# Cross-attention block on one core: scores taken two pairs at a time, context fetched in pieces, the last two pairs' context products placed among output products, and moments turned on chip before they are stored

## The chip, the cores and the metric

The kernel runs on one core of one Trainium2 chip. The metric is the time of one execution in microseconds on the device, as a median over runs. A core has TensorE (PE in the profile, with its weight loads as PEld), VectorE (DVE), ScalarE (ACT), GpSimd (POOL) and SyncE (SP). In this kernel SP issues nearly all the DMAs.

## The reference

A gated cross-attention block followed by a gated feed-forward layer with low-rank adapters. B is 32 sequences, S is 64 tokens, the width is 512, and there are 32 heads of 128.

```python
def xattn(hidden_q, hidden_kv, mask, bias, Wq, Wk, Wv, Wo):
    q, k, v = [(h @ W).reshape(32, 64, 32, 128) for h, W in ((hidden_q, Wq), (hidden_kv, Wk), (hidden_kv, Wv))]
    score = einsum('bqhd,bkhd->bhqk', q, k) / sqrt(128) + bias
    probs = where(mask, softmax(where(mask, score, -inf)), 0)
    return einsum('bhqk,bkhd->bqhd', probs, v).reshape(32, 64, 4096) @ Wo

x = x + tanh(g_xattn[0]) * xattn(layernorm(x), ctx, mask, bias, Wq, Wk, Wv, Wo)
x = x + tanh(g_ffn[0]) * (layernorm(x) @ weight.T + bias_ffn + adapter(layernorm(x)))
```

## The kernel before

Matrix products are done in three terms of rounded halves: each operand is split into a high part (cast by ACT) and a low part (a subtraction on POOL or DVE), and `mm3` (line 98) multiplies high by high, high by low and low by high. The three large projections use a scheme with seven block products in place of eight (`unit`).

The 2048 tokens are worked in two phases of 1024 (`NPH`, index `p`). A phase has two stages. `stage_a` computes K for 16 pairs of heads (`NPR`), then V in four groups; both are stored to DRAM (`kd`, `vd`). Beside it, it takes the moments of the layer norm of x (`x_stats`), stores them with `x_spread` (lines 575 and 576: mean and reciprocal deviation, one float per token, so that a later load can broadcast them along the partitions), and prepares the turned x. `attention` then goes through the 16 pairs in `run`. For pair n it does:

- `unit` on the query weights: seven products of six matmuls, 128x512 each. The results go to `qT`, by ACT copies and DVE additions (lines 354, 359, 376);
- `pv(n - 1)`: the context of the pair before, `po` (line 823), from V and the turned probabilities `pt`. ACT casts it to `ch`, DVE writes the rest `cl` (lines 826, 827);
- `scores(n)`: 64 small matmuls into `ps` (line 765). DVE scales and adds the bias and takes the maximum (767, 769), POOL subtracts the maximum (770), ACT takes the exponential (771);
- `softmax(n)`: DVE sums and inverts (786 to 788), POOL multiplies (789), DVE transposes in blocks of 32 (781), and ACT copies the 16 blocks into `pt` (798);
- `oproj(n - 1, t)`: for eight token tiles, six matmuls 128x512 of `ch` and `cl` with the output weights `wo` into `pa`. DVE adds this to `acc` (847).

Query weights of the next pair are split by `prep`, output weights by `prep_o`, and the mask is added to the bias by `bias_mask` (726). These are Python generators in a list `streams`; each `beat()` after a product issues one step of every one of them, and `drain` issues what is left of one. So the order of instructions on each engine is written by hand (the pool context is under a manual schedule)[...]. Buffers of `big` are named slots: `res[0]` to `res[6]` and `rest`. K of a pair has one slot, V of two pairs has two, `wo` has one, `pt` has one. `sm` (scores of a pair) has two, used by even and odd pairs. [...]

At the end of a phase the last `oproj`s are mixed with other work. In phase 0 this is the first half of phase 1's first K (`plain_half`, `ppk` in the profile), ahead of the last context product. In phase 1 it is the first FFN chunk: `between(t)` puts the FFN's transposes (`tpf`) and their split (`fa`, lines 989 and 990) between output tiles, and `ffn_chunk(0)` begins with the adapter product `pt<-fa,a` (`ffn_lora`, lines 997 and 998). `pt<-tp` is the probabilities and `pt<-fa,a` the adapter product; they share only the name.

## Time and profile before

| what | value |
|---|---|
| runs | 1538.19 us median of 3 (1537.93 to 1539.19) |
| profiled execution, its own time | 1539.96 us |
| its span | 1538.0 us, granted TensorE clock 1.000 |
| PE busy | 1528.1 us (99%), 9000 matmuls |
| DVE, ACT, POOL busy | 963.8, 721.2, 1019.3 us |
| DMA | 248.49 MB, mean 162 GB/s |
| one pair of steady attention, from one `po` to the next | 26.23 us |

Times in the views are microseconds from the start of the span. The busy share of PE is a share of occupied time, and not of peak. In the chain of waits, rows of one engine stand one after the other as they set the end; each row has its start, its length, and how many instructions are merged in it. A row of PE's waits has the instruction, what released it, the total, the number of times and the longest. A timeline row has start, length, engine, line, operation, output and inputs, shapes and count, and in brackets the engine's idle time before and what ended it.

### The profile page before, as it was taken

The page shows a single profiled execution, that of the slowest core. Times are in us where ns is not written, and L with a number is a line of the kernel's source. Part 1 is how long each engine was busy: PE and PEld are TensorE (multiplying, and loading weights), DVE is VectorE, ACT ScalarE, POOL GpSimd, SP SyncE. Part 2 cuts the span into 40 slices and gives each one's busy share as a digit, 9 for nine tenths or more (in the row PEclk, how much of TensorE's full clock was granted, in tenths as well). Part 3 has the DMA queues.
Part 4 walks back from the last instruction along what each step waited for, and adds up shares of the span by engine and source line. Part 5 has one row for each costly group of instructions (what it writes and reads, how often), then busy time and mean ns, then how long its engine had stood idle before and what let it go on. Part 6 is the DMA issues. An engine that isn't in the chain of part 4 may idle for free.

```text
span 1538.0 us, 24845 instructions
## 1 busy us (share of the span) xinstructions
PE 1528.1 (99%) x9000; PEld 1286.0 (84%) x9000; DVE 963.8 (63%) x1595; ACT 721.2 (47%) x1594; POOL 1019.3 (66%) x1128
## 2 busy tenths in 40 slices
PE   9999999999999999999999999999999999999998
PEld 7888888888888888888887888888888888888887
DVE  5665554386666767575675558438666676757764
ACT  6444233345555555556444423334555555555521
POOL 3889478966666657574687947896666665757410
PEclk9999999999999999999999999999999999999999
DMA  5764544384243424441566454438424342444211
GB/s 210 270 183 160 199 164 166 140 298 158 85 176 138 178 83 179 180 152 67 212 240 192 151 199 165 166 137 296 163 85 176 138 176 85 175 182 153 75 42 69
DMA packets 86301, 248.49 MB, mean 162 GB/s; under 512 B 14145, under 2 KB 15169, under 8 KB 77986
## 3 DMA queue, kind: packets, MB, share of 16 engines
q1 hardware_dynamic: 85890, 246.38, 44.6%
q8 instruction: 71, 1.16, 0.3%
q10 hardware_dynamic: 288, 0.52, 0.1%
q14 instruction: 52, 0.43, 0.1%
HBM read 173.45 MB, written 73.42 MB: 161 GB/s over the span
## 4 chain that ended last, share of the span: by engine, by line
PE 93%; DMA 3%; DVE 2%; POOL 1%; issue 1%; ACT 0%; SPq 0%; ACTq 0%; DVEq 0%; POOLq 0%
PE pa L98 22%; PE po L823 7%; PE pzv L98 6%; PE pvv L98 6%; PE pxv L98 6%; PE pzq L98 5%; PE pxq L98 5%; PE pvq L98 5%; PE pzk L98 4%; PE pvk L98 4%; PE pxk L98 4%; PE ps L765 4%; PE pyv L98 3%; PE ppk L98 3%; PE pf L98 3%; PE pyq L98 2%
## 5 line engine op out<-in xcount | busy, mean ns | idle before, releaser
L98 PE MATMUL pa<-wo,ch 128*128 128x512 f32 x1024 | 320.2, 394 | 0.0
L798 ACT COPY pt<-tp 32x256 f32<-32x256 f32 x496 | 200.3, 404 | 87.1 <-DVE tp L781 76.0
L90 POOL TENSOR_TENSOR wo<-rawo,wo 128x512 fp32r<-128x512 f32 x64 | 81.1, 1286 | 224.7 <-ACT wo L89 217.0
L98 PEld LDWEIGHTS pa<-wo,ch 128*128 128x128 f32 x1024 | 189.6, 188 | 39.8
L847 DVE TENSOR_TENSOR acc<-pa,acc 128x512 f32<-128x512 f32 x256 | 170.1, 673 | 79.4 <-PE pa L98 79.3
L98 PE MATMUL pa<-wo,cl 128*128 128x512 f32 x512 | 200.0, 391 | 0.0
L823 PEld LDWEIGHTS po<-pt,v 128*128 128x128 f32 x1024 | 119.1, 192 | 2.6
L827 DVE TENSOR_TENSOR cl<-po,ch 128x512 fp32r<-128x512 f32 x128 | 88.3, 692 | 52.5 <-ACT ch L826 52.0
L823 PE MATMUL po<-pt,v 128*128 128x128 f32 x1024 | 119.4, 275 | 0.0
L98 PEld LDWEIGHTS pa<-wo,cl 128*128 128x128 f32 x512 | 96.2, 188 | 20.6
L826 ACT CAST ch<-po 128x512 fp32r<-128x512 f32 x128 | 74.8, 586 | 71.2 <-PE po L823 70.6
L354 DVE TENSOR_TENSOR vt<-pvv,vt 128x512 f32<-128x512 f32 x64 | 44.1, 689 | 91.5 <-PE pvv L98 91.4
L771 ACT ACTIVATE sm<-sm 128x512 f32<-128x512 f32 x64 | 40.5, 633 | 123.0 <-POOL sm L770 123.0
L770 POOL TENSOR_TENSOR sm<-sm,mx 128x512 f32<-128x512 f32 x64 | 66.9, 1048 | 46.3 <-DVE mx L769 46.3
L354 DVE TENSOR_TENSOR kT<-pvk,kT 128x512 f32<-128x512 f32 x56 | 38.5, 688 | 67.1 <-PE pvk L98 67.1
L376 ACT COPY vt<-pxv 128x512 f32<-128x512 f32 x32 | 18.8, 588 | 131.0 <-PE pxv L98 131.0
L726 POOL TENSOR_TENSOR sm<-sm,madd 128x512 f32<-128x512 f32 x60 | 76.3, 1292 | 1.8 <-DMA sm<-bias 1.8
L789 POOL TENSOR_TENSOR sm<-sm,r 128x512 f32<-128x512 f32 x64 | 66.9, 1045 | 14.5 <-DVE r L788 11.1
L354 DVE TENSOR_TENSOR qT<-pzq,qT 128x512 f32<-128x512 f32 x64 | 44.3, 692 | 38.0 <-PE pzq L98 37.4
L765 PE MATMUL ps<-kB,qT 128*64 128x64 f32 x2048 | 67.2, 224 | 0.3 <-DVE qT L354 0.3
L765 PEld LDWEIGHTS ps<-kB,qT 128*64 128x64 f32 x2048 | 62.5, 138 | 4.9 <-issue 0.7
L354 DVE TENSOR_TENSOR qT<-pvq,qT 128x512 f32<-128x512 f32 x64 | 44.1, 690 | 35.5 <-PE pvq L98 35.5
(975 smaller groups left out, 3698.9 us busy)
## 6 DMA issues: line engine op xcount, KB each, us to landing
kd<-kT SPq DMA_DIRECT2D x64, 512.0 KB, 3.3
vd<-vt SPq DMA_DIRECT2D x128, 256.0 KB, 2.4
kB<-kd SPq DMA_DIRECT2D x32, 1024.0 KB, 4.9
v<-vd SPq DMA_DIRECT2D x32, 1024.0 KB, 9.0
rawq<-wq SPq DMA_DIRECT2D x32, 512.0 KB, 4.6
sm<-bias SPq DMA_DIRECT2D x64, 256.0 KB, 5.2
rawo<-wo SPq DMA_DIRECT2D x32, 512.0 KB, 3.3
rawk<-wk SPq DMA_DIRECT2D x31, 512.0 KB, 5.4
```

The costliest lines, as they stand in the source:

```text
L90: eng.tensor_tensor(lo, raw, hi.bitcast(F32), ALU.subtract)
L98: nc.tensor.matmul(ps, a, b, start=start and i == 0, stop=stop and i == 3 * n - 1, skip_group_check=True)
L354: nc.vector.tensor_tensor(o, ps, i, ALU.add)
L726: nc.gpsimd.tensor_tensor(t, t, masks[p][0], ALU.add)
L765: nc.tensor.matmul(ps[h * S:(h + 1) * S, t, :], qT[:, i, tok], kT[:, i, tok], start=True, stop=True)
L770: nc.gpsimd.tensor_tensor(s, s, mx.unsqueeze(2).to_broadcast([P, NT, S]), ALU.subtract)
L789: nc.gpsimd.tensor_tensor(ss[i], ss[i], r.unsqueeze(2).to_broadcast([P, NT, S]), ALU.mult)
L798: f(pt[dst, i, :, src], of[src, :, ki * 32:(ki + 1) * 32])
L823: nc.tensor.matmul(ps[:, t * P:(t + 1) * P], b["v", n // 2][c][:, t, hg * P:(hg + 1) * P], pt[:, i, c * 4 + t, :], start=True, stop=True)
L826: nc.scalar.copy(ch[:, i, sl], ps)
L827: nc.vector.tensor_tensor(cl[:, i, sl], ps, ch[:, i, sl].bitcast(F32), ALU.subtract)
L847: nc.vector.tensor_tensor(acc[t], ps, acc[t], ALU.add)
```

## The change

Scores of pairs 0 and 1 stay alone. From pair 2 on, `score(a, a + 1)` takes the scores of two pairs in a row; between two such groups stand two `oproj`s, two query `unit`s and two `pv`s, each whole. The exponential becomes a stream step of its own, `normed` and `turned` are the two halves of the old softmax, and for the odd pair of a group they run apart. K has two slots, V has one slot that holds one pair and is loaded anew for each. The last two pairs have `last_turned`: a second tile of probabilities (`pz`), and context products cut in halves (`pv(n, (0,))`, `pv(n, (1,))`) that stand between output tiles, around `fill()`: half a K in phase 0, the first FFN chunk in phase 1. The output weights of pair 14 get a slot of their own. `load_ctx`, `ffn_fetch` and `x1_load` become generators that issue one DMA at a time. `x_spread` turns the moments on DVE and stores them in runs of 32 floats. FFN rows rotate through other buffers. In the diff, cut to its core, the removed lines of the old loop and softmax are left out where they stand in the listing above.

```diff
     def x_spread(p):
         mv, y = mvx[p], rx[p]
-        nc.sync.dma_start(out=lnd[p][0].rearrange("(t q) -> q t", q=P), in_=mv[:, :, 0])
-        nc.sync.dma_start(out=lnd[p][1].rearrange("(t q) -> q t", q=P), in_=y)
+        m, mt = [st.tile([P, 4, NT], F32, tag=f"m{i}", name=f"m{i}{p}", bufs=1) for i in range(2)]
+        for i in range(4):
+            nc.vector.tensor_copy(m[:, i], y if i % 2 else mv[:, :, 0])
+        nc.vector.transpose(mt.rearrange("p a b -> p (a b)"), m.rearrange("p a b -> p (a b)"))
+        for i in range(4):
+            nc.sync.dma_start(out=lnd[p].rearrange("s t (b q) -> b (s t) q", b=4)[i],
+                              in_=mt[i * 32:i * 32 + 2 * NT].rearrange("p a b -> p (a b)"))
...
         def load_k(n):
-            b["k", n] = big(res[1], [P, 2, TP], F32, f"kB{p}_{n}")
+            b["k", n] = big(res[1 + n % 2], [P, 2, TP], F32, f"kB{p}_{n}")
             nc.sync.dma_start(out=b["k", n], in_=kd[p][n])
 
-        def load_v(q):
-            b["v", q] = [big(res[2 + c], [P, 4, 512], F32, f"v{p}_{q}_{c}") for c in range(2)]
-            for c in range(2):
-                nc.sync.dma_start(out=b["v", q][c], in_=vd[p][q][:, c * 4:(c + 1) * 4, :])
+        def load_v(n):
+            b["v", n] = big(res[3], [P, NT, 256], F32, f"v{p}_{n}")
+            nc.sync.dma_start(out=b["v", n], in_=vd[p][n // 2][:, :, n % 2 * 256:(n % 2 + 1) * 256])
...
             load_k(0)
             load_v(0)
+            load_bias(1)
+            load_k(1)
...
             nc.gpsimd.tensor_tensor(s, s, mx.unsqueeze(2).to_broadcast([P, NT, S]), ALU.subtract)
+            beat()
+            if n:
+                streams.append(exped(s))
+            else:
+                nc.scalar.activation(s, s, AF.Exp)
+
+
+        def exped(s):
             nc.scalar.activation(s, s, AF.Exp)
-            beat()
-
...
+        def normed(n, wait):
+            for _ in range(wait):
+                yield
             for i in range(2):
-                nm = f"{p}_{n}_{i}"
-                r = st.tile([P, NT], F32, tag="r", name=f"r{nm}")
-                nc.vector.tensor_reduce(r, ss[i], AX.X, ALU.add)
+                t = sm[n % 2][:, i]
+                r = st.tile([P, NT], F32, tag="r", name=f"r{p}_{n}_{i}")
+                nc.vector.tensor_reduce(r, t, AX.X, ALU.add)
                 nc.vector.reciprocal(r, r)
                 nc.vector.tensor_tensor(r, r, masks[p][1], ALU.mult)
-                nc.gpsimd.tensor_tensor(ss[i], ss[i], r.unsqueeze(2).to_broadcast([P, NT, S]), ALU.mult)
-                if alone and i:
-                    turn(0)
-                yield
-            quads = [(h, qi, ki) for h in range(2) for qi in range(2) for ki in range(2)]
-
-            def copy(f, i, of, h, qi, ki):
-                src = slice(h * 64 + qi * 32, h * 64 + qi * 32 + 32)
-                dst = slice(h * 64 + ki * 32, h * 64 + ki * 32 + 32)
-                f(pt[dst, i, :, src], of[src, :, ki * 32:(ki + 1) * 32])
-
-            if alone:
-                for k, q in enumerate(quads):
-                    copy(nc.scalar.copy, 0, tp[0], *q)
-                    copy(nc.vector.transpose, 1, ss[1], *q)
-                    if k % 3 == 2:
-                        yield
-                return
+                nc.gpsimd.tensor_tensor(t, t, r.unsqueeze(2).to_broadcast([P, NT, S]), ALU.mult)
+                yield
...
+        def turned(n, pace=(1, 2, 2, 3, 2, 2, 2, 2)):
+            tp = []
             for i in range(2):
-                turn(i)
-                yield
+                tp.append(rows.tile([P, NT, S], F32, tag="row", name=f"tp{p}_{n}_{i}"))
+                turn(tp[i], n, i)
+                yield
+            if n + 2 < NPR:
+                load_bias(n + 2)
+                b["m", n + 2] = bias_mask(n + 2)
+                streams.append(b["m", n + 2])
...
+        def last_turned():
+            n = NPR - 2
+            z = kqp.tile([P, 2, NT, S], F32, tag="kq", name=f"tz{p}")
+            tp = [rows.tile([P, NT, S], F32, tag="row", name=f"tp{p}_{n}_{i}") for i in range(2)]
+            pts.append(big(res[1], [P, 2, NT, P], F32, f"pz{p}"))
+            yield from normed(n, 0)
+            for i, _ in enumerate(normed(n + 1, 0)):
+                turn(tp[i], n, i)
+                yield
+            todo = [(n, i, q) for i in range(2) for q in quads]
+
+            def copies(k):
+                for m, i, q in todo[:k]:
+                    copy(nc.scalar.copy, m, i, tp[i] if m == n else z[:, i], *q)
+                del todo[:k]
+
+            for i in range(2):
+                turn(z[:, i], n + 1, i)
+                copies(3)
+                yield
+            for h in range(2):
+                nc.vector.memset(pts[1][h * S:(h + 1) * S, :, :, (1 - h) * S:(2 - h) * S], 0.0)
+                copies(3)
+                yield
+            copies(4)
+
+            def rest():
+                todo.extend((n + 1, i, q) for i in range(2) for q in quads)
+                while todo:
+                    copies(4)
+                    yield
+            b["s", n + 1] = rest()
+            streams.append(b["s", n + 1])
...
+        def pv(n, cs=(0, 1)):
+            drain(b["s", n])
+            for c in cs:
+                for i in range(2):
+                    ps = psum(f"po{p}_{n}_{i}_{c}")
+                    for t in range(4):
+                        nc.tensor.matmul(ps[:, t * P:(t + 1) * P], b["v", n][:, c * 4 + t, i * P:(i + 1) * P],
+                                         pts[n > NPR - 2][:, i, c * 4 + t, :], start=True, stop=True)
+                    sl = slice(c * 512, (c + 1) * 512)
+                    nc.scalar.copy(ch[:, i, sl], ps)
+                    nc.vector.tensor_tensor(cl[:, i, sl], ps, ch[:, i, sl].bitcast(F32), ALU.subtract)
+                    beat()
+            if cs[-1] == 1 and n + 1 < NPR:
+                load_v(n + 1)
+                if ("n", n + 1) in b:
+                    drain(b["n", n + 1])
+                    b["s", n + 1] = turned(n + 1)
+                    next(b["s", n + 1])
+                    next(b["s", n + 1])
+                    streams.append(b["s", n + 1])
...
             raw = raw_of.pop(("o", p * NPR + n))
-            t = big(res[4], [P, 2, 1024], F32R, f"wo{p}_{n}")
+            t = big(res[2 if n == NPR - 2 else 4], [P, 2, 1024], F32R, f"wo{p}_{n}")
...
+            def score(*ns):
+                for n in ns:
+                    drain(b.get(("m", n)))
+                for n in ns:
+                    for i in range(2):
+                        scores(n, i, qT[n], b["k", n])
+                for n in ns:
+                    if n + 2 < NPR:
+                        load_k(n + 2)
+                n = ns[0]
                 if n == 0:
-                    enter_late()
+                    b["s", n] = both(normed(n, 0), first_turned())
+                elif n == NPR - 2:
+                    b["s", n] = last_turned()
                 else:
-                    drain(soft)
-                if 0 < n < NPR - 1:
-                    qb = prep("q", g + 1, nc.gpsimd, 2, 4)
-                    streams.append(qb)
-                if n:
-                    pv(n - 1)
-                    drain(ob)
-                for i in range(2):
-                    scores(n, i, qT, b["k", n])
-                if n + 1 < NPR:
-                    load_k(n + 1)
-                    load_bias(n + 1)
-                    if n % 2 == 0 and n:
-                        load_v(n // 2)
-                soft = softmax(n, None if n == 0 else (1, 2, 2, 3, 2, 2, 2, 2) if n < NPR - 1 or between else (4,) * 4)
-                streams.append(soft)
-                if n:
-                    for t in range(NT - 2):
-                        oproj(n - 1, t)
-                        if n == NPR - 1 and between:
-                            between(t)
-                    drain(qb)
-                    if n + 2 < NPR:
-                        fetch("q", g + 2, "r0")
-                    elif n + 2 == NPR:
-                        before_last()
-                if n == NPR - 5:
-                    prefetch()
-            ob = prep_o(n)
-
-            def finish():
-                oproj(n - 1, NT - 2)
-                oproj(n - 1, NT - 1)
-                streams.append(ob)
-
-            def attend():
-                drain(soft)
-                drain(ob)
-                pv(n)
-            last(finish, attend, lambda t: oproj(n, t), acc)
+                    b["s", n] = both(normed(n, 1), turned(n))
+                streams.append(b["s", n])
+                if 1 < n < NPR - 2:
+                    b["n", n + 1] = normed(n + 1, 5)
+                    streams.append(b["n", n + 1])
+
+            q_unit(0)
+            enter_late()
+            b["m", 1] = bias_mask(1)
+            score(0)
+            streams.append(b["m", 1])
+            start_o(0)
+            q_unit(1)
+            pv(0)
+            start_q(2, nc.gpsimd)
+            score(1)
+            oproj(0)
+            drain(qb[2])
+            fetch("q", p * NPR + 3, "r0")
+            q_unit(2)
+            start_o(1)
+            pv(1)
+            q_unit(3)
+            score(2, 3)
+            for a in range(4, NPR, 2):
+                drain(qb[a])
+                fetch("q", p * NPR + a + 1, "r0")
+                oproj(a - 3)
+                q_unit(a)
+                start_o(a - 2)
+                pv(a - 2)
+                q_unit(a + 1)
+                oproj(a - 2)
+                start_o(a - 1)
+                pv(a - 1)
+                score(a, a + 1)
+                if a == NPR - 8:
+                    streams.append(paced(prefetch(), 4))
+
+            n = NPR - 1
+            oproj(n - 2, range(4), between)
+            fill()
+            oproj(n - 2, range(4, 6))
+            start_o(n - 1)
+            pv(n - 1, (0,))
+            oproj(n - 2, range(6, NT))
+            pv(n - 1, (1,))
+            start_o(n)
+            oproj(n - 1, range(4))
+            drain(ob[n])
+            freed()
+            pv(n, (0,))
+            oproj(n - 1, range(4, NT))
+            pv(n, (1,))
+            last(lambda t: oproj(n, range(t, t + 1)), acc)
...
+            def fill():
+                nonlocal kt0
                 g = (p + 1) * NPR
-                finish()
-                fetch("k", g + 1, "r1")
                 kt0 = k_tile(g)
                 while (2, 1) not in first[1]:
                     next(fb)
                 plain_half(wt["k", g], first[1], k_dst(kt0), f"k{g}", 0)
...
+            def freed():
+                fetch("k", (p + 1) * NPR + 1, "r1")
                 gate.append(True)
...
             def between(t):
-                if 1 <= t < 5:
-                    ffn_tile(0, t - 1)
+                ffn_tile(0, t)
                 if t == 2:
                     ffn_norm(1, 0)
 
-            def last(finish, attend, o, acc):
+            def fill():
+                drain(weights)
+                ffn_chunk(0, first=False)
+
```

## The prediction

> **What bounds the kernel now.** I read the busy times first, then the chain of waits in order of time, then PE's own waits, then the timeline at the places that the change touches.

> ```profile
> PE 1528.1 (99%) x9000; PEld 1286.0 (84%) x9000; DVE 963.8 (63%) x1595; ACT 721.2 (47%) x1594; POOL 1019.3 (66%) x1128
> ```

> PE is busy for 99% of the span, so there is no idle time to win in the middle, only the cost of PE's own work. The chain shows that this cost depends on what follows what (start, length, engine, tile, instructions):

> ```profile
> 683.57 8.41 PE pa L98 x36
> 698.77 2.72 PE pa L98 x12
> 704.21 3.57 PE po L823 x32
> 707.78 2.01 PE ps L765 x64
> 709.80 11.13 PE pa L98 x48
> 720.93 5.44 PE ppk L98 x24
> 726.37 3.57 PE po L823 x32
> 729.94 10.90 PE pa L98 x48
> ```

> The reader is to compare the `pa` rows. Twelve take 2.72 us: 0.2267 us each. 36 should take 8.16 and take 8.41, 48 should take 10.88: behind scores (`ps`) they take 11.13, behind the context product (`po`) 10.90. A change from scores to output products costs 0.25 us, one from `po` to them 0.02. All that PE waited for, beyond a few tenths at the starts, are two waits:

> ```profile
> PE pyk L98 <- POOL wk27p L299: 1.3, 1, 1.3
> PE pt L998 <- DVE fa L990: 1.0, 1, 1.0
> ```

> The first has its cause here (SPq issues; ACT's idle time is in brackets): a 512 KB key weight, issued just ahead of the two DMAs of the moments, lands 12.2 us later.

> ```profile
> 826.84 0.74 SPq L264 DMA_DIRECT2D rawk<-wk  x1
> 827.63 1.19 SPq L575 DMA_DIRECT2D lnd<-mv  x1
> ...
> 839.11 0.41 ACT L295 CAST wk27p<-rawk 128x256 fp32r<-128x256 f32 x1 [6.49 <-DMA rawk<-wk]
> ```

> The others show what one softmax costs its helpers at the end of phase 0, and how DVE's queue held PE before the adapter product of phase 1:

> ```profile
> 716.85 0.70 DVE L781 STREAM_TRANSPOSE tp<-sm 128x512 f32<-128x512 f32 x1
> 717.64 6.82 ACT L798 COPY pt<-tp 32x256 f32<-32x256 f32 x16 [3.10 <-DVE tp L781]
> 725.23 2.51 POOL L90 TENSOR_TENSOR wo<-rawo,wo 128x512 fp32r<-128x512 f32 x2 [7.72 <-issue]
> ```

> ```profile
> 1443.12 0.68 DVE L767 SCALAR_TENSOR_TENSOR sm<-ps,sm 128x512 f32<-128x512 f32 x1
> ...
> 1454.26 0.68 DVE L990 TENSOR_TENSOR fa<-tpf,fa 128x512 fp32r<-128x512 f32 x1
> 1454.99 0.50 PE L998 MATMUL pt<-fa,a 128*128 128x512 f32 x1 [1.03 <-DVE fa L990]
> ```

> ```profile
> kB<-kd SPq DMA_DIRECT2D x32, 1024.0 KB, 4.9
> v<-vd SPq DMA_DIRECT2D x32, 1024.0 KB, 9.0
> ```

> [...]the four `fa` subtractions stand between softmax work in DVE's order, and PE waits for the last. [...]the 4 KB moments, one float at a time, took about 13 us to land. [...]V's new loads have pieces of 1 KB, and no load of before has both that and this size.

> **The change, part by part**, against the profiled span of 1538.0 us. (That execution took 1539.96 in all; the runs' median is 1538.19, 0.2 above the span, so I add the sum to it.)

> *Grouped scores.* Seven groups a phase, 14 in all. Each merges two entries to scores and two exits. An exit costs 0.25. Entry: score starts come 59 ns apart by twos, so 64 are 1.89 us, and the chain gives 2.02: 0.13. The first context product of a group now leads to query products instead: 0.02 back. 14 x 0.36 = **-5.1 us**.

> *Moments turned.* Four copies of 128x8 and one small transpose on DVE (0.15 to 0.7 each; DVE waits for PE here 0.6 at a time) and four DMAs of 128-byte pieces in place of two of 4-byte ones. The weight then lands some 5 us after issue and PE's wait goes: 1.3, with the restart **-1.7 us**. In phase 0 the same delay meets no PE wait.

> *Bit-by-bit fetches* (context, FFN weights, x1) and other buffers for FFN rows: same bytes, needed 30 us later, and a row's store (2.0 us) ends before its buffer's next use 3.7 us on; **0**, hidden by the query and output products; bounds -0.5 and +0.5.

> *Steady groups.* Let T be the end of a group's scores. The even pair's turned weights are wanted at T + 10.9 (outputs) + 9.5 (query) + 0.25 = T+20.7, its second head 0.9 later. DVE: eight score passes at 0.66 from 1.4 us after the first score: done T+2.8. Sums, normalising, transposes between the `acc` additions: second transpose T+9.6. ACT's 16 copies at 0.427 lie between query copies and casts, the last of them behind a POOL sum that stands after the bias additions: T+20.2. **0 us**, with 1.3 us to spare. Wo, bias, K and V have 7 to 40 us.

> *Starts.* Wo's cast and subtraction (1.3 on POOL) now come between pair 0's two normalisings, its last transposes behind, and PE loses two waits for qT of 0.4. Some 0.5 us late in each phase: **+1.0** (bounds -1.5, +4).

> *End of phase 0.* Here the cover shrinks: pair 14's context comes 13.9 us after T (four outputs, 5.44 of key product, two outputs) instead of 20.7, with pair 15's softmax interleaved on DVE. DVE: score passes T+2.8, then four times `acc` 0.67 and a sum with its reciprocal 1.04, a transpose 0.70 in the third and fourth: first transpose T+8.6, second T+11. (Pair 15's transposes and two fills of zeros come later on DVE, where nothing waits for them.) ACT: 16 copies and two key copies (0.58) from T+8.7: T+16.7. PE reaches the second head at 14.8: **+2.0**. Behind this ACT has pair 15's 16 copies, interleaved with context casts and the casts of Wo 14: the second cast ends T+24.2, POOL's second half (1.26) T+25.5. PE wants it at T+23.2 by then, counting the first wait: **+2.4**. The fetch of Wo 15 waits on SP for that POOL instruction (it reads the buffer), and V 15 is queued behind it, since V has one buffer and is loaded only after pair 14's last product. [...]PE needs it after the last 0.5 of output tile 0 and three more at 1.36, 4.6 in all: **+2.1** (0 to 4, as V lands in 4.9 to 7.3).

> *End of phase 1.* The adapter product now follows output tile 3 and its FFN tile directly; before, three output tiles lay between. S is the start of the scores. DVE, in its order: eight passes from S+1.4 to 6.7; `acc` and sum to 8.4; the first `fa` subtraction waits for ACT's four exponentials and cast, 9.2 to 9.9; then three times 0.67 + 1.04 + 0.67, two transposes 1.4, one FFN norm 0.54: S+19.0. PE is there at S + 3.9 + 0.25 + 4 x (1.36 + 0.48) = S+11.5, one product later stands: **+7.2** (5 to 8.5), in place of the old wait of **-1.3**. The FFN chunk then hides pair 14's copies; Wo 14 is late by **+0.9**, V 15 as above **+2.1**.

> Sum: -5.1 - 1.7 + 1.0 + 2.0 + 2.4 + 2.1 + 7.2 - 1.3 + 0.9 + 2.1 = **+9.6 us**, so **1547.8**.

> **The rivals.** (1) *The ends keep up* (faster): it takes an ACT and DVE that run ahead of my queues. For it: in the old phase 0 the 16 copies ended at 724.46, 1.5 us before use. Against: twice the softmax stands in less time. It decides where all waits of ends and starts fall under 5 us; with only 1 us in all: -5.1 - 1.7 - 1.3 + 1 = 1531. (2) *Half of it*: the adapter wait only 5, the chain of Wo 14 and V 15 within its cover: -8.1 + 1 + 2 + 5 = about 1538, no change. (3) *The steady groups stall too*: a bias that lands over a microsecond late holds POOL, its sum, ACT's cast and the last copies; 0.8 us in each of 12 groups gives 1557. (4) *Merging saves less than it says*: if query products after `po` cost 0.25 like outputs after scores, the gain is 14 x 0.13, and the time 1551.

> **How the numbers follow.** 0.2% is 3.1 us, about what a measurement of this kernel can tell from no change. My forecast has 0.64 (own range 1541.5 to 1554), rival 1 has 0.13, rival 2 0.10, rival 3 0.08, rival 4 0.05. Faster 0.13; same 0.09 (most of rival 2); slower 0.78. To hold 8 in 10 the range goes from 1535, below rival 2, to 1556, short of the worst of rival 3.

> **What would show it.** Right: scores of 128 in one block with 0.25 after them once in two pairs; no wait of `pyk`; a PE wait of `pt` for DVE's `fa` of 5 us or more; PE waits of `po` for ACT's `pt`, of `pa` for POOL's `wo`, and of `po` for the V load, at both ends of attention. Wrong: PE waits repeated in every group (rival 3), or PE waits under 5 us in all (rival 1).

## The result, and the profile after

The changed kernel takes **1565.6 us** (median of 6 runs, 1562.0 to 1568.2) against 1538.0 (1537.8 to 1539.2) for the kernel before on the same chip: a ratio of **1.0177** (95% interval 1.0164 to 1.0190), 27.5 us slower. The prediction had the sign right and the size too small: 9.6 us, with a range up to 1556. The profiled execution took 1568.15 us, with a span of 1566.4 where before has 1538.0. It is the slowest of the six, and the profiled execution of the kernel before (1539.96) was 1.9 us above its median too. The comparison of traces below is one of spans: 28.4 us.

First the busy times of the changed kernel:

```profile
span 1566.4 us, 25095 instructions
PE 1531.0 (98%) x9000; PEld 1287.6 (82%) x9000; DVE 963.9 (62%) x1609; ACT 724.9 (46%) x1594; POOL 1020.6 (65%) x1128
```

Work did not grow: DVE, ACT and POOL are within a few microseconds of what they were, and PE has the same 9000 matmuls. The loss is not in what is done, but in when. The steady groups, read from the chain of waits (start, length, engine, tile, instructions), are what was forecast:

```profile
430.59 3.57 PE po L891 x32
434.16 3.88 PE ps L773 x128
438.04 11.13 PE pa L98 x48
458.69 3.57 PE po L891 x32
462.26 1.38 PE pxq L98 x6
```

128 score matmuls in one block, where two blocks of 64 took 2.01 each, and a single `pa` block of 11.13 (0.25 of switching) in two pairs; the first query products behind `po` take 1.38, where six matmuls without a switch take 1.36. From one such `po` row to the next of the same place takes 52.08 us, against 52.46 before. The loss shows in PE's own waits (who waited, for what; us in total, times, longest):

```profile
PE po L891 <- ACT pt L808: 10.7, 7, 2.0
PE po L891 <- DMA v<-vd: 7.6, 2, 4.0
PE pt L1117 <- DVE fa L1109: 5.6, 1, 5.6
PE pvq L98 <- DVE qT L354: 2.4, 2, 1.3
PE pa L98 <- POOL wo L90: 1.6, 2, 0.8
```

Before there was a `pt` of 1.0 and a `pvq` of 0.8; the other rows are new, and `pyk` is gone. To see where they lie, I added up, stage by stage, how much later each matmul starts than the nominal time of the one ahead of it allows (0.2267 us for a 512-column matmul, 0.1116 for `po`, 0.0295 for `ps`). This is PE's loss in us, worked out from the traces, for the two kernels and two of the experiments told below:

| stage | before | after | e10_best | e13_single |
|---|---|---|---|---|
| before the first scores | 3.3 | 3.3 | 4.9 | 3.2 |
| phase 0: 170 us from the first scores | 4.3 | 9.2 | 6.6 | 4.6 |
| phase 0: the other groups | 3.0 | 1.1 | 1.6 | 1.6 |
| phase 0: the end | 0.4 | 10.5 | 0.4 | 0.4 |
| keys and values of phase 1 | 2.1 | 0.1 | 0.1 | 0.1 |
| phase 1: 170 us from the first scores | 4.3 | 9.3 | 6.9 | 4.8 |
| phase 1: the other groups | 3.0 | 1.1 | 1.6 | 1.6 |
| phase 1: the end and the FFN | 3.0 | 16.8 | 4.2 | 5.6 |
| sum | 23.4 | 51.4 | 26.3 | 21.9 |

The difference of the first two sums, 28.0, agrees with that of the spans within 0.4. Five things carry it: 9.9 in the two starts, 10.1 and 13.8 in the two ends, -3.8 in the steady groups, -2.0 at the moments.

Part of the ends isn't waiting. The windows behind three waits (`PEclk` is the last number but two):

```profile
732.00:736.00 4.00, 3.72 (x17) 3.71 (x18) 0.69 (x1) 0.61 (x2) 0.00 (x0) 0.57 0.52 189
1452.00:1459.00 7.00, 4.09 (x12) 3.31 (x13) 3.48 (x8) 0.00 (x0) 1.04 (x1) 0.54 0.00 0
1493.00:1497.00 4.00, 4.00 (x19) 3.68 (x18) 1.38 (x2) 1.17 (x2) 0.00 (x0) 0.57 0.01 4
```

PE's granted clock stood at 0.50 for part of each, which makes the means of 0.57, 0.54 and 0.57. The adapter matmuls behind the longest wait then start 0.43 us apart in place of 0.23. The three stretches at 0.50 last 3.41, 6.83 and 3.41 us, and PE worked for 11.3 us of them. By these 0.43 and 0.23 the same work takes about half as long at full clock, so my estimate of their cost is 5.6 us.

The transfers are later as well (median us from issue to landing):

```profile
kB<-kd SPq DMA_DIRECT2D x32, 1024.0 KB, 9.8
v<-vd SPq DMA_DIRECT2D x32, 1024.0 KB, 7.9
rawq<-wq SPq DMA_DIRECT2D x32, 512.0 KB, 8.7
sm<-bias SPq DMA_DIRECT2D x64, 256.0 KB, 7.0
```

K had 4.9, the query weight 4.6 and the bias 5.2 before. V had 9.0, with its loads issued two at a time.

### The profile page after: what moved, and what is told of

It is laid out like the page before. It is cut to its first block, busy times and chain, and to the rows that moved or that the text cites. A ratio compares the mean times of both kernels' runs of the same rounds, so it can differ in the third digit from the quotient of the medians.

```text
span 1566.4 us, 25095 instructions
## 1 busy us (share of the span) xinstructions
PE 1531.0 (98%) x9000; PEld 1287.6 (82%) x9000; DVE 963.9 (62%) x1609; ACT 724.9 (46%) x1594; POOL 1020.6 (65%) x1128
## 4 chain that ended last, share of the span: by engine, by line
PE 87%; POOL 4%; DVE 3%; DMA 2%; issue 2%; ACT 2%; SPq 0%; DVEq 0%; POOLq 0%; ACTq 0%
PE pa L98 18%; PE po L891 7%; PE pzv L98 6%; PE pvv L98 6%; PE pxv L98 6%; PE pzk L98 5%; PE pvk L98 5%; PE pxk L98 5%; PE pxq L98 5%; PE pzq L98 5%; PE pvq L98 5%; PE ps L773 3%; PE pf L98 3%; PE pyv L98 3%; PE ppk L98 2%; PE pyk L98 2%
## 5 line engine op out<-in xcount | busy, mean ns | idle before, releaser
L98 PE MATMUL pa<-wo,ch 128*128 128x512 f32 x1024 | 320.1, 393 | 2.1 <-POOL wo L90 1.6
L98 PEld LDWEIGHTS pa<-wo,ch 128*128 128x128 f32 x1024 | 190.8, 188 | 43.2 <-POOL wo L90 2.6
L808 ACT COPY pt<-tp 32x256 f32<-32x256 f32 x464 | 187.2, 403 | 67.4 <-DVE tp L811 56.5
L98 PE MATMUL pa<-wo,cl 128*128 128x512 f32 x512 | 199.8, 390 | 0.0
L891 PEld LDWEIGHTS po<-pt,v 128*128 128x128 f32 x960 | 112.3, 192 | 14.9 <-ACT pt L808 12.5
L891 PE MATMUL po<-pt,v 128*128 128x128 f32 x960 | 113.9, 276 | 10.7 <-ACT pt L808 10.7
L98 PEld LDWEIGHTS pa<-wo,cl 128*128 128x128 f32 x512 | 96.2, 188 | 20.3
L90 POOL TENSOR_TENSOR wo<-rawo,wo 128x512 fp32r<-128x512 f32 x64 | 81.4, 1295 | 46.9 <-ACT wo L89 46.8
## 6 DMA issues: line engine op xcount, KB each, us to landing
kB<-kd SPq DMA_DIRECT2D x32, 1024.0 KB, 9.8
v<-vd SPq DMA_DIRECT2D x32, 1024.0 KB, 7.9
```

The source lines that it names most:

```text
L90: eng.tensor_tensor(lo, raw, hi.bitcast(F32), ALU.subtract)
L98: nc.tensor.matmul(ps, a, b, start=start and i == 0, stop=stop and i == 3 * n - 1, skip_group_check=True)
L808: f(pts[n > NPR - 2][dst, i, :, src], of[src, :, ki * 32:(ki + 1) * 32])
L891: nc.tensor.matmul(ps[:, t * P:(t + 1) * P], b["v", n][:, c * 4 + t, i * P:(i + 1) * P], pts[n > NPR - 2][:, i, c * 4 + t, :], start=True, ...
```

## The experiments

My theory after the traces: each late operand has its own late instruction or transfer, and each long wait (4.0, 5.6 and 3.6 us in the trace) also pays for a stretch of half clock; so the losses can be removed one by one, and add. The rival: ACT, DVE and POOL are simply too full at the starts and ends, so that what is removed at one place comes back at the next. In the table, "against after" is the difference of the ratios, times 1538 us; the ratios are to the kernel before on the same chip. These differences are good to some 3 us: the kernel before runs within 1 us of 1538 in part of its executions and up to 5.3 us longer in the others, and its median lay between 1538.0 and 1541.5 from chip to chip. Plain differences of the medians are up to 2.9 us less favourable (2.8 us less than the changed kernel for e9_busy2, in place of 5.7).

| kernel | ratio to before (95%) | us against after |
|---|---|---|
| e1_v15 | 1.0110 (1.0095 to 1.0125) | -10.3 |
| e2_lora | 1.0124 (1.0108 to 1.0141) | -8.2 |
| e3_moments | 0.9992 (0.9983 to 1.0001) | -28.5 (-1.2 against before) |
| e4_starts | 1.0251 (1.0230 to 1.0272) | +11.4 |
| e5_starts2 | 1.0126 (1.0110 to 1.0142) | -7.8 |
| e6_vpair | 1.0122 (1.0108 to 1.0135) | -8.5 |
| e7_busy | 1.0206 (1.0192 to 1.0220) | +4.5 |
| e8_end14 | 1.0092 (1.0078 to 1.0105) | -13.1 |
| e9_busy2 | 1.0140 (1.0126 to 1.0154) | -5.7 |
| e10_best | 1.0015 (1.0007 to 1.0023) | -24.9 |
| e11_split | 1.0021 (1.0013 to 1.0029) | -24.0 |
| e12_late | 1.0120 (1.0103 to 1.0137) | -8.8 |
| e13_single | 0.9997 (0.9988 to 1.0005) | -27.7 |
| e14_lora2 | 1.0023 (1.0013 to 1.0032) | -23.7 |

### e1_v15: the first half of V 15 in a buffer of its own

```diff
-                load_v(n + 1)
+                if n + 1 < NPR - 1:
+                    load_v(n + 1)
+                else:
+                    load_v15(1, big(res[3], [P, 4, 256], F32, f"v{p}_15b"))
...
             copies(4)
+            load_v15(0, rwp.tile([P, 4, 256], F32, tag="r3", name=f"v{p}_15a"))
```

> The changed kernel, but the context tile of pair 15 no longer waits for pair 14's V buffer: the first half of V 15 goes into the freed scores buffer r3 ahead of time, the second half into the V buffer after pair 14's last product. Theory (each wait at the ends is a loss of its own, and a wait of about 4 us also leaves the PE clock at half for some 3.4 us): the waits of po for the V load, 4.1 and 3.8 us, go, with 1.7 and 0.75 us of slow matmuls behind them: 10.3 us less than 1565.6, so about 1555. Rival (the waits only show one common lateness of ACT and POOL at the ends): po then waits for ACT's copies or pa for Wo 15 instead, and at most 3 us are gained, 1562.5 or more.

Measured 1556.3 us, 10.3 less than the changed kernel by the ratios. No wait for V is left in its trace, and the slow stretches behind them are gone (granted clock 0.998 in place of 0.995): the end of phase 0 loses 4.6 in place of 10.5, that of phase 1 11.0 in place of 16.8. The other waits (`pt` for `fa` 5.6, `pa` for `wo` 1.6) kept their size. Nothing came back elsewhere: the V wait was a loss of its own.

### e2_lora: all eight output tiles ahead of the adapter product

```diff
-            oproj(n - 2, range(4), between)
-            fill()
+                oproj(n - 2, range(4), between)
+                oproj(n - 2, range(4, NT))
+                start_o(n - 1)
+                fill()
```

(This in phase 1 alone.)

> The changed kernel, but at the end of phase 1 all eight output tiles of pair 13 stand ahead of the adapter product instead of four. Theory (DVE is late by a fixed time after the scores, so PE has to be given 5.4 us of other work): the waits of pt of 6.7 us fall to about 1.3, and the half clock behind them (2.5 us) goes: 7.9 us less than 1565.6, about 1557.7; phase 0 unchanged. Rival (the additions of those four output tiles on DVE stand before the last fa subtraction, so it comes later by as much): pt still waits 4 us or more, and the time is 1563 or more.

Measured 1558.3 us, 8.2 less. The wait of `pt` fell to 1.1 as expected, but two others came:

```profile
PE pf L1144 <- ACT thl L1132: 2.1, 1, 2.1
PE pt L1124 <- DVE fa L1116: 1.1, 1, 1.1
PE tpf L137 <- DVE xn L132: 1.0, 1, 1.0
PE po L891 <- DMA v<-vd: 1.5, 2, 1.1
```

PE reaches the FFN product of the first tile sooner than ACT, which is among the softmax copies, casts the adapter's result. So the time agrees with the theory for the wrong reason in part: the V waits were shorter in this execution (1.5 us against 7.6), in phase 0 too, where no instruction had moved. There the load took 7.0 us in place of 8.3, and PE came to it later, since a stretch of half clock lay ahead of the wait (at 723.7) and not behind it. In the last phase it took 5.9 in place of 7.9. The spread of the changed kernel's own runs (6 us) fits such a varying load; that it comes from it is not shown.

### e3_moments: the turned moments alone, in the kernel before

The diff is `x_spread` and its DRAM tile, as in the change.

> The kernel before with the turned moments alone. Theory (the 4-byte pieces delay the key weight queued with them): the PE wait of pyk, 1.3 us, goes with the restart behind it: 1536.2 (1.7 to 2.0 less than 1538.0), and the weight rawk lands within 6 us of its issue. Rival (that weight is late for another reason, or the next weight becomes late): 1538.

Measured 0.9992, so -1.2 us, with an interval (-2.6 to +0.2) that just takes in no change. The trace is plain: the wait of `pyk` is gone, K and V of phase 1 lose 0.1 in place of 2.1, and the key weight issued at 827.12 is used by ACT at 832.79:

```profile
827.12 0.72 SPq L264 DMA_DIRECT2D rawk<-wk  x1
832.33 1.71 SPq L580 DMA_DIRECT2D lnd<-m  x4
832.79 0.41 ACT L295 CAST wk27p<-rawk 128x256 fp32r<-128x256 f32 x1
```

So the wait is gone as predicted, and the runs allow a small gain or none. Eleven of its twelve runs took 1537.6 to 1538.5 us, and seven of the fifteen of the kernel before on that chip took 1537.8 to 1538.5, the other eight 1539.9 to 1541.2. That fits a wait of `pyk` which the kernel before has in its longer executions alone; no trace of a shorter one was kept, so this is not shown.

### e4_starts and e5_starts2: the order in the first four pairs

e4_starts moves the bias of pair 2 behind query weight 3, Wo 0 behind pair 0's context, and query weight 4 behind the scores of pairs 2 and 3:

```diff
-            start_o(0)
             q_unit(1)
             pv(0)
+            start_o(0)
...
             score(2, 3)
+            start_q(4, nc.gpsimd)
...
+                if a == 4:
+                    oproj(1)
                 drain(qb[a])
                 fetch("q", p * NPR + a + 1, "r0")
```

> The changed kernel with another order in the first four pairs of each phase and nothing else: the bias of pair 2 is loaded after the query weight of pair 3 instead of before it, the query weight of pair 4 is prepared after the scores of pairs 2 and 3 instead of before them, and Wo 0 is cast after pair 0's context products. Theory (the start waits come from work that stands ahead of the softmax copies in ACT's order, or from a weight queued behind a blocked bias load): the PE losses at 335.5, 364.5, 400.5 and 405.8 us (1.7, 2.0, 1.4, 1.3) go for the most part, in both phases: about 10 us less than 1565.6, so 1555 to 1558. Rival (ACT simply has too much to do in these groups, in any order): the loss moves to other places, 1563 or more.

Measured 1577.1 us, 11.4 **more**: a miss. Wo 0 was now late for its product (waits of 2.9 and 1.9 in each phase, with 6.8 us of half clock behind them), and ACT's cast of query weight 5, fetched later, stood 4.2 us in front of pair 2's copies, so that `po` waited 3.5 there, in place of 1.3. The losses at 364.5 (2.0) and for query weight 4 (1.4) were gone. The two starts lose 14.5 and 14.1. Nor was pair 0's loss of 1.7 touched, though Wo 0 no longer stood between its normalisings: my reading of that place, in the prediction too, was wrong.

e5_starts2 keeps the move of the bias, and makes two others:

```diff
+            for i, _ in enumerate(normed(n, 0)):
+                if i:
+                    turn(tp, n, 0)
+                yield
...
-            q_unit(3)
+            q_unit(3, lambda: load_v(2))
```

> The changed kernel with three small moves in the first four pairs of each phase: the bias of pair 2 is loaded after the query weight of pair 3 (as in e4_starts, where the loss at 364.5 us went), the turn of pair 0's first head is issued in the same step as its second normalising instead of one step later, and V 2 is loaded after the query weight of pair 4 instead of before it. Theory (each start loss has its own late instruction, and in e4_starts the other two moves made new ones): losses of 1.7 (335.5 us) and 2.0 (364.5) go, and of the 2.7 at 400 to 406 about half, in both phases: 7 to 10 us less than 1565.6, so 1556 to 1559. Rival (total work of ACT and DVE in the starts is the limit): less than 3 us, 1563 or more.

Measured 1560.1 us, 7.8 less by the ratios. By its trace the starts gained only 3.2 of this (7.5 and 7.8 in place of 9.2 and 9.3); most of the rest is a V that landed sooner (6.6 and 7.2 us after its issue in place of 8.3 and 7.9). Of the four losses the first went (1.7; small waits for `qT` of 0.75 and 0.5 came, as the kernel before has them), the second halved (1.1 and 1.5), the third fell to 1.0, the fourth (1.3) stayed. Pair 0's loss was one turn issued one step of the planner too late. The second loss is to be seen in the changed kernel's timeline:

```profile
353.97 2.03 SPq L724 DMA_DIRECT2D sm<-bias  x2
356.32 0.33 SPq L264 DMA_DIRECT2D rawq<-wq  x1
360.49 0.41 ACT L295 CAST wq3p<-rawq 128x256 fp32r<-128x256 f32 x1 [2.44 <-DMA rawq<-wq]
366.59 0.60 PE L891 MATMUL po<-pt,v 128*128 128x128 f32 x3 [1.80 <-ACT pt L808]
```

The late query weight held ACT's cast for 2.44 us, and the copies of pair 1's softmax stood behind it in ACT's order: the next two began at 360.80, though their `tp` was turned by 355.64. PE paid 1.80 us at `po`.

### e6_vpair: V in pieces of 8 KB

```diff
-    vd = [[dram.tile([P, NT, 512], F32, name=f"vd{p}_{g}") for g in range(2 * NG)] for p in range(NPH)]
+    vd = [[dram.tile([P, 2, NT, 256], F32, name=f"vd{p}_{g}") for g in range(2 * NG)] for p in range(NPH)]
```

> The changed kernel with V kept in DRAM pair by pair, so that a pair's load has pieces of 8 KB instead of 1 KB and the stores of the value stage pieces of 1 KB instead of 2 KB. Theory (the 1 KB pieces make V and every transfer beside it land later): v<-vd lands within 6 us of its issue instead of 7.9, rawq and kB near 5 again, the waits of po for V fall by 2 us each, and the time falls by 4 to 6 to about 1560. Rival (the landings are later because more transfers are in flight at once, whatever their pieces): landings within 1 us of the changed kernel's, 1564 to 1567.

Measured 1558.9 us, 8.5 less. Landings of e6_vpair:

```profile
kB<-kd SPq DMA_DIRECT2D x32, 1024.0 KB, 9.0
v<-vd SPq DMA_DIRECT2D x32, 1024.0 KB, 6.0
rawq<-wq SPq DMA_DIRECT2D x32, 512.0 KB, 6.7
sm<-bias SPq DMA_DIRECT2D x64, 256.0 KB, 5.0
```

Against the changed kernel V lands 1.9 us sooner, the query weight 2.0 and the bias 2.0. These medians differ between traces: the eight kernels with 1 KB pieces have 7.2 to 7.9, 7.7 to 8.7 and 5.7 to 7.0, the six with 8 KB pieces 5.7 to 6.0, 6.4 to 6.8 and 4.6 to 5.1. The two groups don't overlap, so in these traces the pieces delayed V and what was loaded beside it, by 1 to 2 us. K stays at 9.0: the pieces aren't the main cause there; that it is now issued between other loads may be, but was not tried alone. Both theories had a part of it. The waits for V fell to 3.2 in all, but e2_lora had 1.5 without this edit, so the fall can't be put down to it.

### e7_busy and e9_busy2: work that nobody reads in the long waits

```diff
             oproj(n - 2, range(4), between)
+            if between:
+                busy(48)
             fill()
...
+            busy(30)
             pv(n, (0,))
```

(`busy(k)` multiplies the 128x128 identity with itself k times, into a bank that is not read.)

> The changed kernel with matmuls that nobody reads put into its three long PE waits: 30 of 128x128 before pair 15's context in each phase and 48 before the adapter product. Theory (the wait itself makes the clock fall to half for the matmuls behind it): the late operands come no sooner, but the slow stretches behind the waits go (1.7 + 0.75 + 2.5 us): about 1560.6, granted clock 0.999 or more. Rival (the clock falls for another reason, [...]or recovers as soon as work comes): clock 0.995 and 1565 or more.

Measured 1572.2 us, 4.5 more: the fillers lasted 6.7 and 10.6 us, longer than the waits, since each such matmul is recorded as two here (60 for 30), 0.11 us apart. But behind them the clock was whole (0.999 over the span, in place of 0.995): the 16 context matmuls of pair 15 took 1.71 us in both phases, in place of 3.35 and 2.59. e9_busy2 has half as many.

> As e7_busy with half as many unread matmuls (15 before pair 15's context in each phase, 24 before the adapter product): [...]in e7_busy they lasted 6.7 and 10.6 us where the waits are 4 and 6.7; now 3.35 and 5.3. Theory (a long wait itself halves the clock behind it): no filler outlasts its wait, the slow stretches go as they did in e7_busy (1.7 in phase 0, 2.1 behind the adapter wait, 1.7 behind the last V wait), and the time is 4 to 5.5 us less than the changed kernel's 1565.6, about 1561. Rival (the fillers only take the wait's place, and what the clock gains is lost at the next late operand): 1565 or more.

Measured 1562.8 us, with 108 matmuls more: 5.7 less than the changed kernel by the ratios, 2.8 by the medians. The windows behind the same three waits, in e9_busy2:

```profile
731.00:735.00 4.00, 4.00 (x27) 3.60 (x27) 2.14 (x4) 2.65 (x6) 0.00 (x0) 1.00 0.63 251
1449.00:1456.00 7.00, 5.79 (x32) 4.70 (x31) 3.96 (x9) 1.93 (x4) 1.04 (x1) 1.00 0.00 0
1487.00:1491.00 4.00, 4.00 (x27) 3.56 (x26) 2.08 (x3) 1.17 (x2) 0.00 (x0) 1.00 0.00 0
```

The clock is whole in all three. The adapter's operand came no sooner (its matmuls go on 14.5 us after the last scores in both traces), so for that wait PE's idleness is shown to be what brought the half clock (1.00 in this window, 0.54 in the changed kernel's). The two V loads landed 0.9 and 1.0 us sooner in this execution, which is part of the gain; but e7_busy, whose fillers outlast the V waits, has whole clock behind them too. What the half clock cost is read best from the changed kernel's own trace: by the estimate above, 5.6 of the 28.4 us.

### e8_end14: pair 14's scores ahead of query 15

```diff
                 pv(a - 2)
+                if a == NPR - 2:
+                    score(a)
                 q_unit(a + 1)
...
-                score(a, a + 1)
+                score(*range(a + (a == NPR - 2), a + 2))
```

(And `last_turned` for pair 15 alone, with pair 14's normalising and copies as in a steady group.)

> The changed kernel with its last group of each phase split again: pair 14's scores come before the query product of pair 15, some 24 us earlier, so that at the end only pair 15's softmax is left, and the ends keep their order otherwise. Theory (the ends are late because two softmaxes stand in DVE's and ACT's queues there): the waits of po for pt 14 (1.8), of pt for fa (6.7) and most of those for Wo 14 (1.9 and 0.9) go, with 2.5 us of half clock, against 0.7 for two more entries and exits: 12 to 13 us less than 1565.6, about 1553; the V 15 waits stay. Rival (PE simply reaches these products too early, whatever the softmax): pt still waits 4 us or more, 1560 or more.

Measured 1554.8 us, 13.1 less. At the end of phase 0 the waits for pt 14 and Wo 14 are gone, and the loss is 2.4 in place of 10.5. At the end of phase 1 the theory failed in part: `pt` still waits 5.2 us (3.1 for ACT's cast of `fa`, 1.4 and the rest for DVE's subtraction), since pair 14's copies now stand in ACT's order just there.

### e10_best and e11_split: put together

> The changed kernel with what helped put together: V kept pair by pair (e6_vpair), V 15 in two halves with its first half in freed scores rows (e1_v15), pair 14's scores ahead of query 15 (e8_end14), all output tiles of pair 13 ahead of the adapter product (e2_lora) and the three moves in the starts (e5_starts2). Theory (the losses are separate and add): no PE wait over 1.5 us in attention is left; 1538.0 - 4.4 (grouped scores, twelve groups) - 1.9 (moments) - 1.3 (old adapter wait) + 5 to 7 (what e5_starts2 left in the starts) = 1535 to 1537.5. Rival (the waits share causes, so that the fixes overlap or new waits come): 1541 or more.

Measured 1542.9 us, ratio 1.0015: 24.9 of the 27.2 us are back, but the kernel before isn't reached, and by the time it is the rival (1541 or more). The gains do not add: alone the five parts gave 10.3, 8.2, 7.8, 8.5 and 13.1 us, 47.9 in all, since shorter V waits and the half clock behind them were a share of several. By the trace the theory holds in part: no wait over 1.5 us is left in attention, but the starts still lose 6.6 and 6.9, 2.5 more than before, and new waits around `pf` came (0.9, 0.6 and 1.2). e11_split changes them once more:

```diff
-            q_unit(3, lambda: load_v(2))
-            score(2, 3)
+            score(2)
+            q_unit(3, lambda: load_v(2))
+            score(3)
```

> As e10_best, but pair 2's scores come before the query product of pair 3 and pair 3's after it, so that groups of two begin with pairs 4 and 5. Theory (the start losses at 400 to 406 us come because query weight 4 is prepared between the grouped scores and their copies, with no output products ahead to hide it): the waits for qT 4 and for pt 2, 1.0 and 1.3 in each phase, go for 0.36 more of switching: 3 to 4 us less than e10_best, about 1532.5. Rival (query weight 4 now stands in front of pair 3's softmax instead): within 1 us of e10_best.

Measured 1.0021: the rival. Pair 2's wait went, and `pxq` and `pvq` of pair 3 waited 1.0 and 0.9 for `qT`, whose copy now stood behind pair 2's exponentials in ACT's order.

### e12_late and e13_single: pairs 2 and 3 as before

e12_late gives pairs 2 and 3 single scores with output products between them, and begins the groups at pair 4.

```diff
-            q_unit(3, lambda: load_v(2))
-            score(2, 3)
+            score(2)
+            oproj(1)
+            q_unit(3)
+            start_o(2)
+            pv(2)
+            score(3)
```

> As e10_best, but pairs 2 and 3 keep the order that the kernel before has for every pair (scores of one pair, output products of the pair before, next query product, context), and the groups of two begin with pairs 4 and 5; V 2 is loaded right after pair 1's context again. Theory (what is left in the starts comes from grouping pairs 2 and 3 there with only a query product between the last context and the scores): the losses for qT 4 and pt 2, 1.0 and 1.3 us in each phase, go without a new one (unlike e11_split, where qT 3 came late instead), the PE loss in the first 112 us after the first scores falls from 6.2 to about 4 in each phase, and the time is 4 us less than e10_best's: a ratio of about 0.999 to the kernel before, so 1536 to 1538 where that has 1538. Rival (the turn from single pairs to groups costs this wherever it is put): the waits reappear at pairs 4 and 5, and the ratio stays at 1.0015 or more.

Measured 1557.5 us: a miss, the starts lose 14.1 and 13.8. Wo 1 had only the context product (3.6 us) between its start and its use and came 2.9 late, query weight 4 came 1.9 late, and weight 5 held ACT for 5.1 us. That could not tell the theories apart, so e13_single takes over the rest of the old order:

```diff
+            oproj(0, range(6))
...
             q_unit(2)
+            oproj(0, range(6, NT))
             start_o(1)
...
             score(2)
+            oproj(1, range(6))
+            q_unit(3)
+            oproj(1, range(6, NT))
+            start_o(2)
+            pv(2)
+            score(3)
+            oproj(2, range(3))
+            drain(qb[4])
+            fetch("q", p * NPR + 5, "r0")
+            oproj(2, range(3, 6))
```

> As e12_late, with the order of pairs 0 to 3 taken from the kernel before in full: two output tiles of the pair before stand between a query product and the context, so that Wo has 2.7 us more, query weight 3 is prepared after query product 2, and query weight 5 is fetched among the output products of pair 2. Theory (the starts' loss is that of grouping pairs 2 and 3 without that cover; e12_late moved Wo 1 and query weights 4 and 5 into new waits of 2.9, 1.9 and 1.4): no wait over 0.8 us is left before the first group of two, the PE loss of the first 112 us falls to about 4.5 in each phase, and the ratio to the kernel before is 0.998 to 0.999, about 1535.5 where that has 1538. Rival (the turn from single pairs to groups costs several us wherever it is put): waits of 2 us or more per phase at pairs 4 and 5, ratio 1.002 or more.

Measured 0.9997 (0.9988 to 1.0005), 1538.4 us: level with the kernel before, in a span of 1536.6. All the waits of PE over a few tenths that are left in it:

```profile
PE warm L460 <- POOL ident masks.py:199: 1.3, 1, 1.3
PE pvq L98 <- DVE qT L354: 1.2, 2, 0.6
PE tpf L137 <- DVE xn L132: 1.0, 1, 1.0
PE pzq L98 <- DVE qT L354: 0.7, 2, 0.4
PE pf L1159 <- ACT thl L1147: 0.7, 1, 0.7
```

The starts lose 4.6 and 4.8, near the 4.3 of before, and no wait came up at pairs 4 and 5. The starts' loss therefore belongs to grouping pairs 2 and 3 with too little PE work around them, not to the turn from single pairs to groups; which move of the old order does it was not tried alone. The gain is smaller than expected, in part since the end of phase 1 lost 1.4 more than in e10_best: the waits around `pf` are the same there, but a stretch of half clock (3.4 us at 1442.9) followed them in this execution and not in that one. The two windows at this place in e13_single, then in e10_best (length, PE busy, and the clock as the last number but two; each is as long as one stretch of half clock, and the second of e13_single is that stretch):

```profile
1439.51:1442.93 3.42, 1.78 (x6) 0.71 (x4) 2.42 (x5) 2.52 (x6) 0.00 (x0) 1.00 0.00 0
1442.93:1446.34 3.41, 3.05 (x10) 2.59 (x11) 2.02 (x4) 2.39 (x5) 1.27 (x1) 0.50 0.23 79
1444.02:1447.43 3.41, 2.54 (x10) 1.50 (x8) 2.69 (x5) 1.33 (x3) 0.00 (x0) 1.00 0.00 0
1447.43:1450.84 3.41, 2.27 (x11) 1.80 (x12) 2.32 (x5) 2.80 (x7) 1.29 (x1) 1.00 0.14 49
```

In e13_single PE was idle for 1.64 us of one window, and the next has half clock; in e10_best the same waits fall into two windows, 0.87 and 1.14 of each.

### e14_lora2: pair 14's context behind the adapter product

```diff
         ffn_lora(c)
+        then()
...
-                fill()
-                pv(n - 1, (0,))
+                fill(lambda: pv(n - 1))
```

> As e13_single, with pair 14's context products of phase 1 placed between the adapter product and the FFN output products that use its result, instead of behind these. Theory (what e13_single has left against the kernel before are the waits of pf for ACT's thl and of tpf for DVE's xn, 2.7 us together, and 1.4 to 1.7 us of half clock behind them): 3.4 us of context products cover them, the time is 3 to 4 us less than e13_single's, ratio 0.997 to 0.998 to the kernel before. Rival (the context products come before their softmax is turned, or ACT's casts of their results come before thl): a new wait of 2 us or more there, ratio 0.999 or more.

Measured 1.0023: a miss. The waits of `pf` went, and `tpf` waited 5.6 us for DVE's `xn` in their place. DVE's timeline in e14_lora2 has the reason: four context subtractions, each waiting for an ACT cast that stands among pair 15's copies, come in front of the FFN norm.

```profile
1442.25 0.69 DVE L884 TENSOR_TENSOR cl<-po,ch 128x512 fp32r<-128x512 f32 x1 [0.32 <-ACT ch L883]
1444.22 0.69 DVE L884 TENSOR_TENSOR cl<-po,ch 128x512 fp32r<-128x512 f32 x1 [1.28 <-ACT ch L883]
...
1449.56 0.54 DVE L132 TENSOR_SCALAR xn<-x1t,mv,yf 128x512 f32<-128x512 f32 x1
```

## Why the prediction was right and wrong

- **Grouped scores, -5.1: right in size.** The period of two pairs fell by 0.38 us (0.36 forecast; 14 of these are 5.0, not 5.1), where groups run steadily. No wait appeared in the steady groups: rival 3 is out. So is rival 4: the chain has `po` followed by query products at 3.57, without a switch.
- **Moments, -1.7: the mechanism was right.** 2.0 in the traces, 1.2 (from 2.6 to none) in the runs of e3_moments. I took the wait from an execution of 1539.96 us and set the gain against a median of 1538.19, whose executions may not have that wait.
- **Bit-by-bit fetches, 0:** no wait of PE for them is in the trace; they weren't tried alone.
- **Starts, +1.0 (bounds -1.5 and +4): the step that failed most.** They cost 9.9 in both phases together: four losses in each, of 1.7 (pair 0's turn), 2.0 (query weight 3, late), 1.4 (`qT` 4) and 1.3 (pair 2's copies), where the kernel before has two of 0.6. I costed one thing, Wo's cast between pair 0's normalisings, and e4_starts shows that even this was not what made pair 0 late (e5_starts2: a turn issued one step too late was). Query weights 3 and 4, their casts in ACT's order, and the grouping of pairs 2 and 3 with nothing but a query product ahead of it were not costed at all: "Wo, bias, K and V have 7 to 40 us" left the query weights out, and used landings of before. The query weight's rose from 4.6 to 8.7.
- **Pair 14's second head, +2.0, and Wo 14, +2.4 and +0.9: right.** Measured 1.8, then 2.1 (in three pieces) and 0.9. e8_end14, with pair 14's softmax out of the way, has neither at the end of phase 0.
- **V 15, +2.1 twice: the mechanism was right, the size wrong.** 4.1 and 3.8 in the profiled execution, 1.3 and 0.5 in that of e2_lora. I let V land 6.7 us after POOL's last instruction on Wo 14, 5.3 of it for V's own landing; only the 4.9 of a lone K stood in a trace, and the rest was my estimate. The two loads took 8.3 and 7.9 (in the chain of waits, with the context products behind them):

```profile
723.87 8.28 DMA v<-vd
732.28 3.65 PE po L891 x16
...
1484.55 7.94 DMA v<-vd
1492.62 2.94 PE po L891 x16
```

In six other traces with the same pieces they took 5.9 to 7.3, with 8 KB pieces (e6_vpair) 5.8 and 6.0. What the 1 KB pieces added no trace of before showed; the measure is e6_vpair's, 1 to 2 us.
- **Adapter product, +7.2 (5 to 8.5) for the old 1.3: right.** PE lost 6.7 there: 5.9 for DVE's subtraction and 0.8 for ACT's cast. e2_lora shows the order to be the cause.
- **The clock: missing.** No step of the sum had the half clock behind a long wait. It is 1.7 behind V 15 in phase 0, 2.2 behind the adapter and 1.7 behind V 15 in phase 1: 5.6 us (e9_busy2 gained 2.8 to 5.7 without it). The trace that I forecast from could not show it: its granted clock is 1.000 and its longest wait of PE 1.3 us. I had forecast a wait of 7.2 us, beyond anything in that trace, and charged it at its length alone.

The sum, in the terms of the prediction: starts 8.9 too little, clock 5.6, V 15 3.7; with the 9.6 forecast that makes 27.8, where the table of losses has 28.0. Rival 1 (the ends keep up) and rival 2 (half of it) fall with the waits seen. In rival 1 the old copies are said to end 1.5 us before their use; they ended 1.9 before it (724.46 and 726.37).

## What to carry to other kernels

A change of order has to be costed over every helper queue at its beginning and end, where the steady cover is missing, with each operand that PE takes there, the weights of the next stage among them; the landings of before did not hold here once loads were split and crowded (the query weight's went from 4.6 to 8.7 us). Count a long PE wait as more than its length: those of 4.0, 5.6 and 3.6 us here had half clock behind them, and by my estimate it cost 1.7, 2.2 and 1.7 us more. And when waits are mended by moving work, expect the next one: of 14 kernels here four moved the loss instead of removing it. Five repairs together brought most of it back, and the last step down to the old level was to take the old order back wherever groups had no cover.
